# Two small float32 matmuls of an attention turned into float32r ones

## The chip, the core and the metric

One core of a Trainium2 chip runs the whole program. The metric is the device time of one execution in microseconds (us). Each engine has its own list of instructions and works through it in order; semaphores make one engine wait for another. PE is TensorE (PEld its weight loads), DVE is VectorE, ACT is ScalarE, POOL is GpSimd, SP issues DMAs. PE reads SBUF and writes PSUM alone.

## The reference, cut to what matters

Two perceiver layers on x (8 batches x 64 rows x 512), with a context of 8 x 1601 x 512. The change lies in the first attention of the first layer (32 heads of 128, 8 KV heads):

```python
q = (query @ Wq + bq).reshape(B, L, NKV, G, HDIM)
k_, v_ = jnp.split(kv @ Wkv + bkv, 2, axis=-1)
...
scores = jnp.einsum('blkgd,bmkd->bkglm', q, k) * scale
attn = jax.nn.softmax(scores, axis=-1)
o = jnp.einsum('bkglm,bmkd->blkgd', attn, v).reshape(B, L, NHEAD * HDIM)
return o @ Wo + bo
```

After it come a state-space block (mamba), a ternary linear layer, a second attention to the context, a causal self-attention and a gated feed-forward layer, each added to x.

## The kernel before, in words

**Units.** The first attention runs over 64 units, a unit being a pair (batch b, KV head i). A unit has 4 heads x 64 rows = 256 query columns and 1601 keys in 13 blocks of 128 (the last of 65). `x_all` (L517) writes out their order by hand, in six steps s = 0..5 per unit: in step s the current unit gets key projections (`x_k`, L354), value projections (`x_v`, L319) and scores (`x_s`, L369), while the unit before it gets its maximum (s = 0), exponentials (`x_exp`), values (`x_av`, L454) and at s = 5 its output (`x_o`). Two units are thus under way at any time. A scheduler then orders each engine's list from this text by its own model of the time; each list is fixed before the program runs.

**Precision.** Most matrices are held as a pair hi, lo of float32r tiles. `split` (L100) makes them: ACT copies the source to hi (L105, or L108 with a bias), another engine subtracts hi from the source for lo (L106, L109). A product is then three float32r matmuls (hi hi, hi lo, lo hi). Some small matmuls are float32 instead; among them are the two in question, the products of the exponentials with the values (L464) and parts of the mamba.

**The maximum.** Scores stand with keys on partitions and queries along the columns. `x_s` copies them from PSUM to an S tile (ACT, L388) and keeps an elementwise maximum `mx` over the key blocks (DVE, L392, L395). `x_max` (L397) transposes `mx` on PE (L403) into PSUM tile `m_ps`, and DVE reduces it to the column `mc` of negated maxima, one for each query (L405). `x_spread` (L408) brings it back along the columns on all partitions: for each of the two halves of 128 queries, a matmul with the column, broadcast, as the stationary operand and the identity as the moving one (L412), 128 columns wide, in float32. `x_exp` adds the spread maximum to S (DVE, L426) and takes the exponential (ACT, L427).

**The sum.** POOL adds up the exponentials into `ss` (L429, L452, L446) and its two halves into `sl` (L448), which holds a partial sum for each partition. In the very last unit (`flush`) DVE does part of it (L434 to L442). `x_o` (L466) adds over the partitions and spreads the result with one float32 matmul with a matrix of ones, 256 columns wide, into the second half of PSUM tile `o_ps` (L472). The reciprocal follows (L474 to L477), then the product with the values (L479), bias and split (L485).

**Buffers that matter.** PSUM: `kv` has four buffers for k_ps, v_ps, s_ps and w_ps, `o_ps` one, `m_ps` one. SBUF: `ss`, `sl`, `mx` and `rw` one each, `S` eleven, `mc` two. Pool `xw` holds the two `x1` tiles in which a pair of batches' result is gathered (`x_wo`, L492).

**Beside it.** Side work is fed into the units at given rates: splitting weights (`halves`), preparing the later layers (`prep`), and the later layers themselves for four groups of two batches (`chain`). Its DVE, ACT and POOL instructions are pinned in program order, which is why many have the line L65. The last group's chain, with what is left of the third group's, runs alone at the end. `consts` (L147) makes the identity (POOL) and the ones at the start.

Of the kernel before, what the change touches and what calls it, by code (L numbers as in the profile page):

```python
# [8 lines left out]
FP = mybir.dt.float32  # L9
FR = mybir.dt.float32r  # L10
AF = mybir.ActivationFunctionType
ALU = mybir.AluOpType
# [4 lines left out]
P = 128  # L17
D = 512
# [60 lines left out]
class Kernel:  # L79
# [67 lines left out]
    def consts(self):  # L147
        nc, i = self.nc, self.i
        c = self.ctx.enter_context(self.tc.tile_pool(name="const", bufs=1))
        self.c = c  # L150
        self.ident = c.tile([P, P], FP, name="ident")
        make_identity(nc, self.ident)
        self.eps5 = c.tile([P, 1], FP, name="eps5")
        nc.gpsimd.memset(self.eps5, 1e-5)
        self.ones = c.tile([P, P], FP, name="ones")
        nc.gpsimd.memset(self.ones, 1.0)
        self.eps6 = c.tile([P, 1], FP, name="eps6")
        nc.gpsimd.memset(self.eps6, 1e-6)

        def ld(name, shape):  # L160
            t = c.tile(shape, FP, name="c_" + name)
            nc.sync.dma_start(out=t, in_=i[name])
            return t

        self.bq = ld("bq", [P, 32])
        self.bk = ld("bk", [P, NKV])
        self.bv = ld("bv", [P, NKV])
# [229 lines left out]
    def x_max(self, b, i):  # L397

        nc = self.nc
        m = self.mf.pop((b, i))  # L400
        ps = self.px.tile([P, 2, 256], FP, name=self.nm("m_ps"), tag="m", bufs=MB)
        for h in range(2):
            nc.tensor.transpose(ps[:, 0, h * P : (h + 1) * P], m[:, 0, h * P : (h + 1) * P], self.ident)  # L403
        col = self.sb("mc", [P, 2], pool=self.xp, bufs=2)
        nc.vector.tensor_reduce(col, ps[:, 0].rearrange("p (h k) -> p h k", k=P), AX.X, ALU.max, negate=True)  # L405
        self.mm[(b, i)] = (ps, col)

    def x_spread(self, b, i):  # L408

        ps, col = self.mm[(b, i)]  # L410
        for h in range(2):
            self.nc.tensor.matmul(  # L412
                ps[:, 1, h * P : (h + 1) * P], lhsT=col[:, h : h + 1].to_broadcast([P, P]), rhs=self.ident, start=True, stop=True
            )

    def x_exp(self, b, i, n):

        nc = self.nc
        ps = self.mm[(b, i)][0]
        S = self.S[(b, i)]  # L420
        if n == 0:
            self.ss[(b, i)] = self.sb("ss", [P, 2, 256], pool=self.xp, bufs=1)
        ss = self.ss[(b, i)]
        r, w = (P, 2) if n < 6 else (TAIL, 1)
        sv = S[n][:r, :w]
        nc.vector.tensor_tensor(sv, sv, ps[:r, 1:2].to_broadcast([r, w, 256]), ALU.add)  # L426
        nc.scalar.activation(sv, sv, AF.Exp, scale=ISC)  # L427
        if n == 1:
            nc.gpsimd.tensor_tensor(ss, S[0], S[1], ALU.add)  # L429
        elif n > 3 and self.flush:  # L430

            if n == 5:
                t = self.fs = self.sb("rw", [P, 256], pool=self.xp, bufs=1)
                nc.vector.tensor_tensor(t, S[4][:, 0], S[4][:, 1], ALU.add)  # L434
                for k in range(2):
                    nc.vector.tensor_tensor(t, t, S[5][:, k], ALU.add)
            elif n == 6:
                t = self.fs
                nc.vector.tensor_tensor(t[:r], t[:r], sv[:, 0], ALU.add)
                l = self.sb("sl", [P, 256], pool=self.xp, bufs=1)  # L440
                nc.vector.tensor_tensor(l, ss[:, 0], ss[:, 1], ALU.add)
                nc.vector.tensor_tensor(l, l, t, ALU.add)  # L442
                self.l[(b, i)] = l
                self.mm.pop((b, i))
        elif n == 6:
            nc.gpsimd.tensor_tensor(ss[:r, 0], ss[:r, 0], sv[:, 0], ALU.add)  # L446
            l = self.sb("sl", [P, 256], pool=self.xp, bufs=1)
            nc.gpsimd.tensor_tensor(l, ss[:, 0], ss[:, 1], ALU.add)  # L448
            self.l[(b, i)] = l
            self.mm.pop((b, i))  # L450
        elif n > 1:
            nc.gpsimd.tensor_tensor(ss, ss, S[n], ALU.add)  # L452
# [13 lines left out]
    def x_o(self, b, i):  # L466

        nc = self.nc
        ps = self.o.pop((b, i))
        self.S.pop((b, i))  # L470
        r = self.l.pop((b, i))
        nc.tensor.matmul(ps[:, 1], lhsT=self.ones, rhs=r, start=True, stop=True)  # L472
        w = self.sb("rw", [P, 256], pool=self.xp, bufs=1)
        nc.scalar.activation(r, ps[:, 1], AF.Ln)  # L474
        nc.scalar.activation(r, r, AF.Exp, scale=-1.0)
        nc.vector.tensor_tensor(w, ps[:, 1], r, ALU.mult)
        nc.vector.scalar_tensor_tensor(r, w, 2.0, r, ALU.subtract, ALU.mult, reverse0=True)  # L477
        oa = w
        nc.vector.tensor_tensor(oa, ps[:, 0], r, ALU.mult)  # L479

        odd = b % 2
        oav = oa.rearrange("p (g t) -> p g t", t=T)
        scr = self.ot_s[b // 2][i]
        ot = self.sb("ot", [P, 2, G, 2, T], FR, pool=self.xp, bufs=OTB)
        self.split(ot[:, 0, :, odd], ot[:, 1, :, odd], oav, bias=self.bv[:, i : i + 1])  # L485
        if odd:
            nc.sync.dma_start(out=ot[:, :, :, 0].bitcast(FP), in_=scr)
            self.ot[(b, i)] = ot
        else:
            nc.sync.dma_start(out=scr, in_=ot[:, :, :, 0].bitcast(FP))  # L490
# [794 lines left out]
    def run(self):  # L1285
        nc, tc, ctx = self.nc, self.tc, self.ctx
# [2 lines left out]
        self.pc = ctx.enter_context(tc.tile_pool(name="pc", bufs=2, space=PSUM))  # L1289
        xctx = ctx.enter_context(ExitStack())  # L1290
        self.px = xctx.enter_context(tc.tile_pool(name="px", bufs=2, space=PSUM))
        self.consts()
        self.scratch()
        self.xw = ctx.enter_context(tc.tile_pool(name="xw", bufs=2))
        self.xp = xctx.enter_context(tc.tile_pool(name="xp", bufs=2))
        qctx = ctx.enter_context(ExitStack())
        self.q_ln(qctx.enter_context(tc.tile_pool(name="qp", bufs=2, side="right")))
# [192 lines left out]
```

## Time and profile before

| | |
|---|---|
| three timed runs, median (lowest to highest) | 2689.3 us (2683.2 to 2691.5) |
| the profiled execution | 2687.2 us, its span 2685.1 us |
| mean granted PE clock in it | 0.983 |
| first L472, last L472 | 108.4 us, 2375 us |
| L403, transposes of mx (PE) | 128 records, 25.3 us, 274 ns each |
| L405, reduction to mc (DVE) | x64, median 418 ns |
| L448, sum l (POOL) | x63, median 738 ns |
| L452, additions of exponentials (POOL) | x254, 349.3 us, median 1290 ns |
| L474, logarithm of the sum (ACT) | x64, median 386 ns |
| PE's idle time before L472 | 0.0 us |
| PE's idle time before L412 | 3.0 us, until DVE's mc |
| DVE's idle time before L426 | 20.5 us, of which 20.2 until PE's L412 |

How to read it. A row of a group gives the count, the busy time as the union of its instructions, the mean of one in ns, and the idle time of the engine just before them with what ended it. Matmuls overlap on PE: the mean of one record includes its drain, the busy time of a group does not count the overlap twice. A row of the chain gives the start in us, the length in us, and the engine, tile and line; "x12" counts records. A stage's row gives busy us and the count of each engine, then the granted clock of PE, the share of the DMA engines and their GB/s.

### The profile page before, as it was taken

To read this page: it belongs to the slowest core of one execution; us is meant where nothing else is said; L and a number is where in the kernel's file an instruction comes from. 1 tells how busy PE (TensorE), PEld (TensorE's weight loads), DVE (VectorE), ACT (ScalarE), POOL (GpSimd) and SP (SyncE) were. 2 spreads that over 40 slices of the span, in tenths; PEclk is the share of its full clock that TensorE was granted. 3 is DMA by queue.
4 is the path that set the end of the run, shared out by engine and by line. 5 is a ranking of instruction groups with operands and counts; after the bars stand their busy time and mean duration, and the time that the engine had idled before them with its cause. 6 is when DMAs were issued, how large, how long until landed. Compare 5 with 4: busy or idle time off the path is not lost.

```text
span 2685.1 us, 43976 instructions
## 1 busy us (share of the span) xinstructions
PE 2549.7 (95%) x16320; PEld 2269.3 (85%) x16320; DVE 1667.6 (62%) x2739; ACT 1350.2 (50%) x3128; POOL 1247.6 (46%) x1243
## 2 busy tenths in 40 slices
PE   7999999999999999999999999999999999977797
PEld 6988999999999899978989988988898898964544
DVE  4534357665687775545567676554657777668754
ACT  4545454344556554544555554544546545436433
POOL 2434463463368663521367457521239556405420
PEclk9999999999999999999999999999999999987899
DMA  9788876675213244764324452665343455466674
GB/s 308 225 295 276 281 239 190 203 240 180 67 66 105 68 133 150 232 190 145 97 98 148 149 161 89 216 201 164 102 135 92 137 159 155 143 226 216 234 261 166
DMA packets 311126, 466.08 MB, mean 174 GB/s; under 512 B 88440, under 2 KB 187768, under 8 KB 306432
## 3 DMA queue, kind: packets, MB, share of 16 engines
q1 hardware_dynamic: 310912, 463.28, 53.4%
q8 instruction: 128, 2.10, 0.3%
q14 instruction: 86, 0.70, 0.1%
HBM read 389.66 MB, written 73.53 MB: 173 GB/s over the span
## 4 chain that ended last, share of the span: by engine, by line
PE 68%; DMA 9%; DVE 9%; POOL 7%; issue 4%; ACT 3%; SPq 0%; POOLq 0%; DVEq 0%; ACTq 0%
PE v_ps L334 16%; PE k_ps L363 16%; PE o_ps L464 10%; PE s_ps L385 8%; POOL a L65 3%; PE w_ps L511 2%; PE acc L274 2%; DVE a L65 2%; PE acc L1077 2%; PE acc L801 2%; PE acc L1021 1%; PE acc L759 1%; PE acc L756 1%; POOL ss L452 1%; DMA b<-in_ctxT_dram 1%
## 5 line engine op out<-in xcount | busy, mean ns | idle before, releaser
L363 PE MATMUL k_ps<-cxb,wk 128*128 128x384 f32 x2304 | 470.3, 347 | 35.3 <-DVE mx L392 13.2
L334 PE MATMUL v_ps<-wv,cxb 128*128 128x256 f32 x3456 | 467.9, 281 | 1.0 <-DVE kt L109 0.6
L334 PEld LDWEIGHTS v_ps<-wv,cxb 128*128 128x128 f32 x3456 | 438.0, 188 | 19.3 <-issue 11.7
L363 PEld LDWEIGHTS k_ps<-cxb,wk 128*128 128x128 f32 x2304 | 405.3, 191 | 53.2 <-DVE mx L392 15.6
L464 PE MATMUL o_ps<-S,v 128*128 128x256 f32 (+1 forms) x1664 | 413.6, 381 | 7.4 <-DVE rw L479 4.0
L385 PE MATMUL s_ps<-q,kt 128*128 128x256 f32 (+1 forms) x2496 | 413.7, 299 | 5.2 <-DVE mx L392 2.4
L385 PEld LDWEIGHTS s_ps<-q,kt 128*128 128x128 f32 (+1 forms) x2496 | 342.8, 185 | 28.5 <-issue 6.9
L388 ACT COPY S<-s_ps 128x512 f32<-128x512 f32 (+1 forms) x448 | 241.9, 553 | 241.0 <-PE s_ps L385 236.6
L452 POOL TENSOR_TENSOR ss<-ss,S 128x512 f32<-128x512 f32 x254 | 349.3, 1375 | 14.7 <-ACT S L427 1.3
L392 DVE TENSOR_TENSOR mx<-s_ps,mx 128x512 f32<-128x512 f32 x256 | 175.1, 684 | 264.0 <-ACT S L388 262.7
L464 PEld LDWEIGHTS o_ps<-S,v 128*128 128x128 f32 (+1 forms) x1664 | 298.6, 190 | 46.7 <-issue 5.2
L429 POOL TENSOR_TENSOR ss<-S,S 128x512 f32<-128x512 f32 x64 | 84.5, 1320 | 469.4 <-ACT S L427 469.1
L108 ACT ACTIVATE kt<-k_ps,c_bk 128x384 fp32r<-128x384 f32 (+1 forms) x256 | 152.0, 594 | 246.9 <-PE k_ps L363 245.9
L426 DVE TENSOR_TENSOR S<-S,m_ps 128x512 f32<-128x512 f32 (+1 forms) x448 | 257.3, 640 | 20.5 <-PE m_ps L412 20.2
L427 ACT ACTIVATE S<-S 128x512 f32<-128x512 f32 (+1 forms) x448 | 246.7, 599 | 43.4 <-DVE S L426 42.7
L109 DVE SCALAR_TENSOR_TENSOR kt<-k_ps,c_bk,kt 128x384 fp32r<-128x384 f32 (+1 forms) x256 | 160.9, 629 | 158.0 <-ACT kt L108 156.5
L337 ACT COPY v<-v_ps 128x256 f32<-128x256 f32 (+1 forms) x416 | 152.5, 368 | 198.4 <-PE v_ps L334 196.0
L334 PE MATMUL v_ps<-wv,cxt 128*128 128x256 f32 (+1 forms) x1536 | 206.5, 282 | 1.5 <-DVE mx L392 1.0
L334 PEld LDWEIGHTS v_ps<-wv,cxt 128*128 128x128 f32 (+1 forms) x1536 | 192.7, 175 | 10.5 <-issue 3.4
L65 DVE TENSOR_TENSOR_SCAN a<-a,a 128x512 f32<-128x512 f32 x96 | 154.7, 1613 | 62.9 <-POOL a L65 62.8
L363 PE MATMUL k_ps<-cxt,wk 128*128 128x450 f32 x768 | 178.6, 375 | 1.4 <-DVE mx L392 1.3
L65 POOL TENSOR_TENSOR a<-a,bc 128x512 f32<-128x512 f32 x96 | 128.1, 1335 | 90.7 <-DVE a L65 90.7
(357 smaller groups left out, 3947.8 us busy)
## 6 DMA issues: line engine op xcount, KB each, us to landing
wo<-d_wo SPq DMA_DIRECT2D x128, 512.0 KB, 5.3
wk<-d_wk SPq DMA_DIRECT2D x63, 512.0 KB, 3.5
wv<-d_wv SPq DMA_DIRECT2D x31, 1024.0 KB, 5.7
cst<-in_ctxT_dram SPq DMA_DIRECT2D x96, 192.0 KB, 3.0
b<-in_ctxN_dram SPq DMA_DIRECT2D x36, 512.0 KB, 3.7
d_q<-q_t SPq DMA_DIRECT2D x32, 512.0 KB, 5.9
q<-d_q SPq DMA_DIRECT2D x64, 256.0 KB, 3.1
d_wo<-wo SPq DMA_DIRECT2D x32, 512.0 KB, 5.7
```

What stands on the lines that cost most here:

```text
L65: return lambda *a, **k: self.tc.keep_in_program_order(f(*a, **k))
L109: eng.scalar_tensor_tensor(lo, src, bias, hi.bitcast(FP), ALU.add, ALU.subtract)
L334: nc.tensor.matmul(ps[:r], lhsT=cx[:, a, c, o : o + r], rhs=w[:, m, c, :], start=k == 0, stop=k == 11)
L337: nc.scalar.copy(vt[:r], ps[:r])
L363: nc.tensor.matmul(ps[:, :wd], lhsT=w[:, a, c, :], rhs=cx[:, m, c, :], start=k == 0, stop=k == 11)
L385: nc.tensor.matmul(sp[:r, gi, :], lhsT=kt[:, a, o : o + r], rhs=q[:, m, :], start=k == 0, stop=k == 2)
L388: nc.scalar.copy(s[:r, :n], sp[:r, :n])
L392: nc.vector.tensor_tensor(mx, sp, S[0] if len(S) == 1 else mx, ALU.max)
L426: nc.vector.tensor_tensor(sv, sv, ps[:r, 1:2].to_broadcast([r, w, 256]), ALU.add)
L427: nc.scalar.activation(sv, sv, AF.Exp, scale=ISC)
L452: nc.gpsimd.tensor_tensor(ss, ss, S[n], ALU.add)
L464: nc.tensor.matmul(ps[:, 0], lhsT=self.v[(b, j, t)][:r, hc : hc + P], rhs=S[t // 2][:r, t % 2], start=t == 0, stop=t == NT - 1)
```

## The change

Three parts. The column `mc` becomes a float32r tile, and L412 multiplies it by a float32r view of the identity. The sum l is split into float32r halves hi and lo (ACT's copy, then POOL's subtraction; DVE's in the last unit), and `x_o` adds them up by two float32r matmuls with ones that accumulate in the same PSUM tile. hi and lo take a new tile with the tag `ss`, of which there is one buffer. So that identity and ones exist in float32r, the identity is made in a tile of pool `xw` and copied by ACT; the ones are made from it by DVE. Float32 users see both through a bitcast. Pool `xw` is opened earlier for that.

```diff
+        one = self.xw.tile([P, D], FP, name="one", tag="x1")[:, :P]
+        make_identity(nc, one)
+        self.ident_r = c.tile([P, P], FR, name="ident")
+        self.ident = self.ident_r.bitcast(FP)
+        nc.scalar.copy(self.ident_r, one)
...
+        self.ones_r = c.tile([P, P], FR, name="ones")
+        self.ones = self.ones_r.bitcast(FP)
+        nc.vector.tensor_scalar(self.ones_r, self.ident, 0.0, 1.0, ALU.mult, ALU.add)
...
-        col = self.sb("mc", [P, 2], pool=self.xp, bufs=2)
+        col = self.sb("mc", [P, 2], FR, pool=self.xp, bufs=2)
...
-                ps[:, 1, h * P : (h + 1) * P], lhsT=col[:, h : h + 1].to_broadcast([P, P]), rhs=self.ident, start=True, stop=True
+                ps[:, 1, h * P : (h + 1) * P], lhsT=col[:, h : h + 1].to_broadcast([P, P]), rhs=self.ident_r, start=True, stop=True
...
+                sr = self.ss[(b, i)] = self.sb("ss", [P, 2, 256], FR, pool=self.xp, bufs=1)
+                self.split(sr[:, 0], sr[:, 1], l)
...
+            sr = self.ss[(b, i)] = self.sb("ss", [P, 2, 256], FR, pool=self.xp, bufs=1)
+            self.split(sr[:, 0], sr[:, 1], l, eng=nc.gpsimd)
...
-        nc.tensor.matmul(ps[:, 1], lhsT=self.ones, rhs=r, start=True, stop=True)
+        sr = self.ss.pop((b, i))
+        for h in range(2):
+            nc.tensor.matmul(ps[:, 1], lhsT=self.ones_r, rhs=sr[:, h], start=h == 0, stop=h == 1)
```

## What was predicted

> **What bounds the kernel now.** I read the page's busy times first, then the busy time by stage, the chain of work that ended last in order of time, and the groups by line and shape for the two kinds of matmul that the change touches.
>
> ```profile
> span 2685.1 us, 43976 instructions
> PE 2549.7 (95%) x16320; PEld 2269.3 (85%) x16320; DVE 1667.6 (62%) x2739; ACT 1350.2 (50%) x3128; POOL 1247.6 (46%) x1243
> ```
>
> TensorE (PE) is busy for 95% of the span and the next engine, VectorE, for 62%. That is a mean over stages, so here are stages, as "busy (instructions)" of PE, weight loads, DVE, ACT and POOL:
>
> ```profile
> 400.00:800.00 400.00, 396.81 (x2658) 377.81 (x2657) 270.44 (x484) 190.79 (x420) 184.20 (x187) 1.00 0.50 158
> 1600.00:2000.00 400.00, 390.30 (x2547) 347.59 (x2547) 236.82 (x402) 195.22 (x458) 161.34 (x162) 1.00 0.47 153
> 2376.00:2686.00 310.00, 244.66 (x1344) 155.66 (x1344) 200.14 (x378) 141.81 (x377) 89.91 (x97) 0.88 0.67 226
> ```
>
> From 400 to 2000 us PE idles about 2% and ACT and POOL have half their time left. Matmul time saved in the first attention should therefore be time saved, as long as nothing new makes PE wait. The last 310 us have no first attention in them, and PE idles there for a fifth.
>
> ```profile
> L412 PE MATMUL m_ps<-ident,mc 128*128 128x128 f32 x256 | 40.0, 277 | 3.0 <-DVE mc L405 3.0
> L472 PE MATMUL o_ps<-sl,ones 128*128 128x256 f32 x128 | 38.2, 380 | 0.0
> ```
>
> Each of the 64 units (batch, KV head) issues two float32 matmuls on L412 and one on L472. That is 128 and 64, and the rows count 256 and 128: a float32 matmul leaves two records. The last number but one is the length of one record with its drain, which overlaps the next, so it is no price. A price is the spacing in a dense run; the chain in order of time gives it as start, us, what, records:
>
> ```profile
> 1484.19 2.11 PE k_ps L363 x12
> ...
> 1936.42 2.73 PE v_ps L334 x24
> ...
> 2223.84 2.16 PE o_ps L464 x10
> ...
> 2525.34 2.68 PE acc L941 x24
> ```
>
> float32r with 256 columns (L334): 2.73/24 = 114 ns each; with 384 (L363): 2.11/12 = 176. float32 with 256 columns (L464): 2.16/10 = 216 a record, 432 a matmul. float32 with 128 columns (L941): 2.68/24 = 112 a record, 224 a matmul.
>
> **The change part by part.**
>
> *The sum (L472).* Per unit one float32 matmul of 256 columns (432 ns) becomes two float32r ones of 256 (2 x 114 = 228). 204 ns x 64 = **13.1 us** less PE time.
>
> *The spread (L412).* Per unit two float32 matmuls of 128 columns (2 x 224) become two float32r ones of 128. No float32r matmul narrower than 256 columns is in the trace. From above its price is 224, if it gains nothing. From below it is half of L334's 114, 57: from 256 to 384 columns the price grows in proportion. Between them stands the weight load, which does not shrink with the columns streamed: a load record takes 188 ns for 128 columns (L472) and 134 for 65 (the last s_ps of a unit), so 63 columns cost 54 ns and 128 cost some 110. No two 128x128 matmuls or transposes in a run lie closer than 108 ns (L403, L412). I take 110, the row nearest in shape. Saving: 114 ns x 128 = **14.6 us**, ends 0 and 21.4.
>
> A rule that would price this otherwise is in the Trainium skill, "TensorE: Matmul & The Clock Gate", section "Back-to-back issue gap": a sustained stream of weight loads and matmuls is put there at about 81 ns per matmul for 128 columns and 131 for 512. By 81 this part would save 18.3 us (an estimate from that page) instead of 14.6. The same rule's 131 ns for 512 columns does not agree with this trace, where dense L274 matmuls of 512 columns start 228 ns apart, so I keep the row.
>
> *The split, and PE's wait for it.* After L448 (the sum l, on POOL), ACT copies l to hi (L474, same shape, 386 ns) and POOL subtracts (like L448, 738), some 1.3 us with hand-offs, then both matmuls. Paired in time, l ended before L472 began by 0.4 to 23 us, median near 10; four units have under 1.3 us (0.40, 0.77, 1.21, 1.23), nine under 2.5. The order of the built programs puts the pair of matmuls where L472 stood among first-attention matmuls for 57 of 64 units. With 1.3 us the shortfall is some 1.6 us in all, with 2.5 (a queue in front of each step) some 9. I take **3 us lost**. POOL's 63 x 738 = 47 us and ACT's 64 x 386 = 25 us of new work fit into their idle half.
>
> *ACT held up.* The copy waits for POOL, and ACT takes its list in order: behind it stand S<-s_ps, v<-v_ps and kt<-k_ps (L388, L337, L108), for which PE's ring of four "kv" buffers waits. I laid the new ACT order over the old times. In the first 32 units ACT reaches the copy before l is there 22 times, mostly by 0.1 to 3.7 us, once by 9; the next ACT instruction would start late by 22 us in all, 8 of it in unit 22. Doubled for 64 units: 44 us at worst. The ring holds three more groups of 0.7 to 2.1 us of matmuls, which covers delays up to about 3 us, so all but the longest are hidden. I take **5 us lost**, ends 0 and 44.
>
> *The ring of one for ss.* hi and lo take the ss buffer, so the next unit's first addition (L429) waits for both matmuls. In the trace L429 starts 7 us or more after the previous L472 in 61 of 63 pairs; twice it is 1 to 3 us ahead of it. POOL is not the bound: nothing.
>
> *The start.* The identity now passes through ACT. POOL has it at 1.5 us, ACT's table load ends at 2.0, the copy can end before 2.5; x arrives at 4.9 us and the first transpose is at 13.7. Nothing. Moving pool xw earlier shifts addresses alone. One "x1" buffer is used once before its first real use, long released.
>
> *The last unit.* Its sum is on DVE; L472 waits 1.6 us behind an L758 that waits for a DMA, which covers copy and subtraction (0.4 + 0.4). Nothing.
>
> *What moves.* 36 matmuls of the third group's chain, ahead of the last unit's L472 before, now stand behind it: 20 float32r ones of 512 columns (228 ns) and 16 float32 of 128 (224), 8.2 us. They leave the full stage for one in which PE has a fifth free, so the effect lies between -8.2 and, if they delay that chain instead, about +8. I take 0.
>
> **Sum:** -13.1 - 14.6 + 3 + 5 = -19.7 us. The profiled execution took 2687.2 us (span 2685.1), 2 us below the median of the three timed runs, 2689.3. 2687.2 - 19.7 = 2667.5; I predict **2667 us**. About 0.3% (8 us) is what a measurement of this kernel can tell from no change.
>
> **Rivals.**
>
> 1. *The narrow float32r matmul gains nothing* (224 ns at 128 columns). For it: no row shows a narrow one. Against: the prices of 256, 384 and 512 columns are in proportion. It gives 2687.2 - 13.1 + 8 = 2682, within 0.3%.
> 2. *ACT's line becomes the bound: slower.* Its place is the copy of l to hi; every instruction behind it on ACT waits for POOL's slow additions (1.29 us each), and PE runs out of its four buffers. It decides once PE loses more than 27.7 us by it. At the worst end, 44 us, with the 3 of the late matmuls, it gives 2687.2 - 27.7 + 47 = 2706. For it: ACT would wait in two of three units. Against: most of these waits are shorter than what the ring covers, and the order was not the same in the later units.
> 3. *Everything hides:* 57 ns, no stalls, and the moved matmuls fall into idle time: 2687.2 - 13.1 - 21.4 - 8.2 = 2644.
>
> **Chances.** The forecast (2655 to 2679) 0.58; rival 1 0.19; rival 2 0.16; rival 3 0.07. Faster by over 0.3% is forecast and rival 3, 0.65; within 0.3% rival 1, 0.19; slower by over 0.3% rival 2, 0.16. The range, 2650 to 2690, takes in the forecast and rival 1 and leaves out most of rivals 2 and 3.
>
> **What would show it.** L472's line should have 128 records 114 ns apart, and L412's 128 instead of 256. If L412's pairs lie about 110 apart the spread is right; at 224, rival 1. Idle time of PE before L472 "until POOL" is the late split. Idle time of ACT that ends with POOL's sl, together with PE waits on "ACT S" or "ACT kt", is rival 2. The stages from 400 to 2000 us should stay 97% full on PE with fewer us in each. The prediction is wrong if PE's idle time before 2376 us grows by more than 8 us, or if the last stage becomes longer than 310 us.

## The result and the profile after

The changed kernel takes **2694.5 us** (median of 13 runs, 2689.5 to 2700.4); the kernel before, on the same chip, 2688.3 us (13 runs). The ratio is 1.0024, 95% interval 1.0015 to 1.0034: no gain, and if anything a small loss, where 2667 us was predicted. The profiled execution took 2697.6 us.

Line numbers have moved by four to ten: L412 is now L416, L448 is L454, L464 (values) L472, L472 (the sum) L482, L511 L521, L759 L769, L801 L811, L812 L822. The page's total, then its stages:

```profile
span 2695.6 us, 43902 instructions
PE 2543.5 (94%) x16192; PEld 2256.3 (84%) x16192; DVE 1681.6 (62%) x2741; ACT 1371.3 (51%) x3193; POOL 1290.5 (48%) x1305
```

The 128 records fewer are the spread's: the change is in. But PE's busy time fell by only 6 us. The stages, columns as before (busy us and count of PE, PEld, DVE, ACT, POOL, granted clock, DMA share, GB/s):

```profile
400.00:800.00 400.00, 394.84 (x2645) 376.33 (x2644) 276.70 (x488) 196.74 (x440) 192.97 (x200) 1.00 0.49 157
1600.00:2000.00 400.00, 392.52 (x2580) 350.73 (x2579) 234.21 (x396) 200.43 (x474) 171.37 (x177) 1.00 0.47 148
2000.00:2376.00 376.00, 344.47 (x2145) 307.94 (x2144) 257.39 (x379) 189.66 (x466) 218.58 (x228) 0.96 0.43 136
2376.00:2696.00 320.00, 249.67 (x1337) 156.74 (x1336) 200.73 (x374) 141.28 (x374) 89.40 (x97) 0.85 0.66 219
```

And the third of these stages in the kernel before:

```profile
2000.00:2376.00 376.00, 357.05 (x2287) 324.73 (x2285) 261.35 (x381) 193.38 (x470) 221.29 (x227) 0.99 0.44 137
```

Up to 2000 us all is as predicted: PE as full as before, and further along. In the third stage PE has 142 matmuls fewer to do and is busy for 12.6 us less; that time is now idle, and nothing has moved into it. The two lines of the change, and the copy to hi, in groups by line and shape:

```profile
L482 PE MATMUL o_ps<-ss,ones 128*128 128x256 f32 x128 | 28.2, 290 | 2.1 <-ACT ss L105 1.3 <-POOL ss L106 0.6
L105 ACT CAST ss<-sl 128x256 fp32r<-128x256 f32 x64 | 25.9, 405 | 82.0 <-POOL sl L454 81.9
L416 PE MATMUL m_ps<-ident,mc 128*128 128x128 f32 x128 | 22.4, 255 | 1.1 <-DVE mc L409 0.9
```

The two matmuls of L482 wait 2.1 us in all for the split, and ACT waits 82 us in front of its copy. The price of a pair is read from the starts of matmuls: from the first record of the pair to the start of the sixth matmul behind it, less the usual spacing of the five between, median over the units with no gap. That takes in what the follower pays.

| per unit | before | after | difference x 64 |
|---|---|---|---|
| sum (L472, then L482) | 426 ns | 241 ns | -11.8 us |
| spread (L412, then L416) | 454 ns | 226 ns | -14.6 us |

Together -26.4 us, where -27.7 was predicted. Other choices of the usual spacing change each price by some 10 ns. Within a pair the starts are not where the prediction looked for them: the two L482, where they are neighbours, start 121 ns apart (median), the two L416 only 60 ns. The matmul after the second L416 then starts 112 ns behind it, and the one after that comes some 55 ns later than usual, so 226 ns is the price of the pair and not a spacing.

Gaps of over 0.3 us between matmul starts, beyond the usual spacing, from 80 us to the last sum, add up to 55.8 us before and 60.7 after: 5 us lost, where 8 was predicted. The sums depend on what is taken as usual (other choices give 63 to 88 us), and the loss lies between 0 and 7 us. By these numbers the first attention should end some 20 to 26 us earlier; its last sum starts at 2346.1 us instead of 2375.3, 29 us earlier (52 records of side work, of 1468, went behind it). **The whole gain is there at 2346 us.** From the last sum to the end, the kernel before needs 310 us and the changed one 349.5.

What happens there, in order of time (start us, us, engine, line, idle time of the engine before it and its releaser), in the changed kernel; these are chosen rows, with others between them:

```profile
2360.47 0.69 DVE L524 TENSOR_TENSOR x<-w_ps,x 128x512 f32<-128x512 f32 x1 [10.70 <-PE w_ps L521]
...
2368.49 0.63 PE L768 MATMUL acc<-w,a 128*128 128x512 f32 x1
2371.81 0.80 PE L768 MATMUL acc<-w,a 128*128 128x512 f32 x1 [1.84 <-DMA w<-d_wout]
2375.61 0.79 PE L768 MATMUL acc<-w,a 128*128 128x512 f32 x1 [2.15 <-DMA w<-d_wout]
2379.12 0.79 PE L768 MATMUL acc<-w,a 128*128 128x512 f32 x1 [1.86 <-DMA w<-d_wout]
2379.71 0.63 PE L769 MATMUL acc<-w,a 128*128 128x512 f32 x1
2380.45 0.21 POOL L822 MEMSET xpad<- 128x6 f32 x4 [40.06 <-PE acc L769]
2380.99 0.68 DVE L141 BATCH_NORM_STATS2 ln_st<-x 128x6 f32<-128x512 f32 x1
2386.23 3.65 PE L811 MATMUL acc<-a,w 128*128 128x128 f32 x22
```

L524 gives the last group's x, the end of the first attention: ready at 2361.2. Its next reader, the layer norm (L141), starts at 2381.0, and the last group's chain multiplies from 2386.2. What it waits for shows on POOL: a memset (L822), which reads nothing, waits 40 us for PE's L769. That is the third group's mamba, the last matmul of its out-projection (L766 to L769), which ends at 2380.3. A memset can only wait for the memory it writes. Once the first attention is over, a new pool `tp` opens for the last stage in the place of pool `ca`, which held the mamba's tiles: `actx.close()`, then `tile_pool(name="tp")` in `run`. So the last group's chain waits for the third group's mamba. (On DVE, L141 also stands in the list behind an addition of the third group that waits for the same L769; the experiments on memory below tell the two apart.) In the kernel before, the same two instructions:

```profile
2384.91 0.21 POOL L812 MEMSET xpad<- 128x6 f32 x4 [7.62 <-DMA b<-in_ctxT_dram]
2385.56 0.69 DVE L141 BATCH_NORM_STATS2 ln_st<-x 128x6 f32<-128x512 f32 x1
```

There the mamba ended at 2375.2 and x was ready at 2385.5: x was later, by 10 us. The DMA that this row names as the releaser landed just before the memset, but it need not be the one waited for: the last matmul of the first attention (L511) had ended too, and DVE's addition to x, which waits for that one, starts at 2384.83, 0.08 us before the memset. After the change, where both wait for L769, the memset starts as closely behind DVE's instruction (0.07 us, 2380.45 against 2380.38). So L511 fits as well; in the built programs the matmul that the memset waits for is this L511 before, and the mamba's last L769 after.

After the change x is 24 us earlier, and the mamba 5 us later. It does not follow the units: the last 16 of the mamba's 32 scans on DVE start 8 to 14 us later than before, while the units beside them run 26 to 34 us earlier. And its end is not PE's work. In the chain of work that ended last (start us, us, what), of the stretch from 2340 to 2392 us:

```profile
2345.24 2.63 DMA w<-d_wout
...
2369.15 2.62 DMA w<-d_wout
2371.77 0.04 issue
2371.81 0.81 PE acc L768
2372.62 0.02 issue
2372.64 2.93 DMA w<-d_wout
2375.57 0.04 issue
2375.61 0.81 PE acc L768
2376.42 0.02 issue
2376.44 2.64 DMA w<-d_wout
```

Load a slice of the weight, multiply for 0.8 us, free the buffer, load the next. The same view gives DMA w<-d_wout 20.8% of this stretch. Meanwhile PE is busy for half of the time and DVE for a quarter; the stretch from 2346 to 2386 us:

```profile
2346.00:2386.00 40.00, 20.87 (x73) 14.20 (x73) 10.33 (x28) 6.28 (x19) 1.47 (x5) 0.64 0.53 170
```

### The profile page after: what moved, and what is told of

Read it like the earlier page. It is cut to its first block, busy times and chain, and to the rows that moved or that the text cites. A ratio compares the mean times of both kernels' runs of the same rounds, so it can differ in the third digit from the quotient of the medians.

```text
span 2695.6 us, 43902 instructions
## 1 busy us (share of the span) xinstructions
PE 2543.5 (94%) x16192; PEld 2256.3 (84%) x16192; DVE 1681.6 (62%) x2741; ACT 1371.3 (51%) x3193; POOL 1290.5 (48%) x1305
## 4 chain that ended last, share of the span: by engine, by line
PE 64%; DVE 10%; DMA 9%; POOL 9%; issue 5%; ACT 3%; SPq 1%; POOLq 0%; DVEq 0%; ACTq 0%
PE v_ps L338 15%; PE k_ps L367 15%; PE o_ps L472 9%; PE s_ps L389 8%; POOL a L65 3%; DVE a L65 3%; PE w_ps L521 2%; PE acc L278 2%; POOL ss L460 2%; PE acc L1087 2%; PE acc L811 2%; PE acc L1031 2%; PE acc L766 2%; PE acc L769 1%; DMA wo<-d_wo 1%
## 5 line engine op out<-in xcount | busy, mean ns | idle before, releaser
L367 PE MATMUL k_ps<-cxb,wk 128*128 128x384 f32 x2304 | 463.7, 343 | 31.0 <-DVE mx L396 11.3
L338 PEld LDWEIGHTS v_ps<-wv,cxb 128*128 128x128 f32 x3456 | 440.5, 189 | 26.4 <-issue 16.3
L367 PEld LDWEIGHTS k_ps<-cxb,wk 128*128 128x128 f32 x2304 | 399.0, 190 | 48.4 <-issue 11.5
L472 PE MATMUL o_ps<-S,v 128*128 128x256 f32 (+1 forms) x1664 | 413.0, 381 | 1.6 <-DVE rw L489 1.6
L472 PEld LDWEIGHTS o_ps<-S,v 128*128 128x128 f32 (+1 forms) x1664 | 300.5, 190 | 36.6 <-DVE rw L489 2.0
```

The source lines that it names most:

```text
L338: nc.tensor.matmul(ps[:r], lhsT=cx[:, a, c, o : o + r], rhs=w[:, m, c, :], start=k == 0, stop=k == 11)
L367: nc.tensor.matmul(ps[:, :wd], lhsT=w[:, a, c, :], rhs=cx[:, m, c, :], start=k == 0, stop=k == 11)
L472: nc.tensor.matmul(ps[:, 0], lhsT=self.v[(b, j, t)][:r, hc : hc + P], rhs=S[t // 2][:r, t % 2], start=t == 0, stop=t == NT - 1)
```

## The experiments

What the expectations call theory A: the third group's chain keeps a pace of its own, and the last stage is held by its mamba, so that TensorE time freed in the first attention is not time saved. Rivals are named in each. All times are medians; a ratio is to the kernel before on the same chip and in the same call, whose medians lie between 2687.7 and 2691.0 us.

### Each part alone

Here e1_spread keeps the float32 sum, e2_sum the float32 spread, and e3_consts has only the new way to make identity and ones.

```diff
 # e1: the column and L416 as in the change, L472 and its sum as before
 # e2: the split and L482 as in the change, L412 and mc as before
 # e3: only consts() and the earlier opening of pool xw
```

> The spread by float32r alone, the sum as before. Theory A (the first attention gets shorter, but the third group's mamba, which runs beside it and is not bound by TensorE, keeps its own pace, and the end of the program hangs on it): the last sum matmul comes some 14 us earlier than in the kernel before (2361 against 2375 us), the time stays within 5 us of 2688. Theory B (the split's copy and subtraction, with ScalarE and GpSimd waiting for each other, slow that mamba; less TensorE work alone is a gain): 2672 to 2677 us. Theory C (any edit moves the scheduler's order, and the order alone moves the end by some us): no pattern with the edit.

> The split sum alone, the spread in float32 as before. Theory A: the last sum matmul 13 us earlier (2362), the time within 5 us of 2688. Theory B: slower than the kernel before, 2692 to 2702 us, since it has all of the added waits and half of the saving. Theory C: no pattern.

> Only the constants made as in the change (identity through ScalarE, pool opened earlier), the attention as before. Theories A and B: 2688, within 2 us. Theory C: it differs by more than 4 us, for it too gives the scheduler another text.

e1 takes 2705.0 us, 1.0055 (1.0040 to 1.0070); e2 2718.2, 1.0109 (1.0092 to 1.0125); e3 2689.2, 1.0002 (0.9992 to 1.0012). The constants cost nothing, as predicted. The prices hold alone: the spread 228 ns a unit in e1, the sum 241 in e2. Yet both are slower, outside the ranges of theories A and B, and e1 adds no work in the units. The third group's mamba ends at 2391.9 us in e1 and 2400.4 in e2, against 2375.2 before, and from there to the end of the span it is 311 and 322 us, against 310 before: the end follows the mamba, as theory A says, but theory A did not foresee a later mamba. Why it ends later still than in the whole change was not settled.

### ACT's wait taken away

The copy to hi moves to POOL, which has made l itself, so ACT no longer waits for it.

```diff
-            self.split(sr[:, 0], sr[:, 1], l, eng=nc.gpsimd)
+            nc.gpsimd.tensor_copy(sr[:, 0], l)
+            nc.gpsimd.tensor_tensor(sr[:, 1], l, sr[:, 0].bitcast(FP), ALU.subtract)
```

> The whole change, but GpSimd makes both halves of the sum (copy, then subtraction), so ScalarE no longer waits for GpSimd's sum nor GpSimd for ScalarE's copy. Theory B: ScalarE's 82 us of waiting for the sum go, and the time falls to 2670 to 2682 us. Theory A: 2688 to 2700 us, as the whole change. GpSimd has some 0.7 us more work for each of 63 units.

2694.3 us, 1.0012 (1.0000 to 1.0024), the time of the change itself. The ss tile's waits in the changed kernel (engine, tile, line: us, times):

```profile
  POOL sl L454: 81.9, 48
```

In e4 this line is gone (one copy is left on ACT, of the last unit), and nothing is gained at the end. That alone does not clear ACT's line (rival 2 of the prediction), for e4's first attention ends later than the change's: its last sum starts at 2365.6 us, with 44 more records of side work ahead of it, and one wait of 9.7 us on PE. What speaks against rival 2 is the changed kernel itself, whose PE loses 0 to 7 us in the units where that rival needs over 27.7. For theory A e4 is a point: the last sum moves by 19 us against the change and the end does not, while the mamba ends at 2377.3 us (2380.3 in the change) and the last chain starts 6 us behind it.

### The rate of the third group's chain

`SPAN` holds the due time of each group's chain, in batches of the first attention; the third's goes from 2.6 to 2.5 or 2.4, with and without the change; e12 takes all three down.

```diff
-SPAN = [3.1,3.1,2.6,0.2]
+SPAN = [3.1,3.1,2.5,0.2]
```

> The whole change, with the third group's chain fed in over 2.5 instead of 2.6 batches, so that its mamba stands some 20 us earlier in the lists. Theory A (the last group's chain can start only when that mamba has ended, and the end follows it by 305 to 322 us, whatever the first attention does): mamba end near 2360 instead of 2380, the time 2668 to 2682 us. Theory D (the last stage is bound by the work left to it, and what is moved ahead lengthens the units by as much): within 5 us of 2694.

> The kernel before over 2.5 batches. There the mamba's end (2375 us) and the first attention's last projection (2385 us) nearly coincide, so under theory A little is to be had: 2680 to 2692 us. Theory D: the same. If it falls to 2670, the gain of the whole change with this setting is not the change's.

> The same over 2.4 batches. Theory A: the mamba ends before the first attention does (2350 to 2360 us), the time 2655 to 2675 us. Theory D: within 8 us of 2694.

> The kernel before over 2.4 batches. Theory A: 2675 to 2692 us, above the whole change at the same setting by some 15 us or more.

> The whole change with the chains of all three groups fed in somewhat faster (3.0, 3.0 and 2.5 batches instead of 3.1, 3.1 and 2.6). Theory A: the mamba's end moves ahead to about 2350 to 2360 us and the time falls below the kernel before, 2670 to 2685 us. Theory C: any value from 2680 to 2720.

At 2.5 the changed kernel takes 2687.0 us, 0.9992 (0.9983 to 1.0000), and its control 2700.4, 1.0036 (1.0023 to 1.0048): the change is now worth 13 us. At 2.4 both are slow: 2719.1, 1.0104 (1.0088 to 1.0119), and 2728.1, 1.0139 (1.0125 to 1.0153). e12 takes 2728.3, 1.0145 (1.0117 to 1.0172). All five lie above the ranges of theory A. One reason is that a smaller `SPAN` does not mean an earlier mamba: it ends at 2360 us at 2.5, but at 2381 (e6) and 2385 at 2.4, and at 2404.6 in e12, where 2350 to 2360 was expected of e6 and e12. The other is that the expectation of a fixed 305 to 322 us from the mamba's end to the end of the span, which the kernel before, the changed one, e1, e2 and e9 kept, did not hold in e5 to e8 (327 to 341).

### Less TensorE work by another road

e9 is the kernel before with the last of the twelve matmuls of each value block left out (L333): 416 matmuls of 114 ns, some 48 us of PE. Neither the sum nor the spread is touched.

```diff
-            for a, m in ((0, 0), (0, 1), (1, 0)):
+            for a, m in ((0, 0), (0, 1), (1, 0))[: 2 if c == NC - 1 else 3]:
```

> The kernel before, with the last of the 12 matmuls of every value block left out (lo times hi of the last quarter of the contraction): 416 x 116 ns = 48 us less TensorE work in the first attention and nothing added anywhere. Theory A (the side chain keeps its own pace and sets the end): the last sum matmul some 48 us earlier (2327), the time no more than 15 us less (2673 to 2690). Rival E (the units' matmul time does bound the kernel, and the change lost its gain to what it adds): 2638 to 2652 us.

2694.3 us, 1.0007 (0.9994 to 1.0019). Its last sum starts at 2337.2 us, 38 earlier than before, and its x is ready 32 us earlier, at 2353.0; nothing of it arrives at the end. The same two readings as after the change:

```profile
2374.70 0.21 POOL L812 MEMSET xpad<- 128x6 f32 x4 [42.73 <-PE acc L759]
2375.24 0.68 DVE L141 BATCH_NORM_STATS2 ln_st<-x 128x6 f32<-128x512 f32 x1
```

The mamba ends at 2374.6 us, within 1 us of the kernel before (2375.2), and the memset waits 43 us for it. The last chain starts at 2380.6 us, only 11 us before that of the kernel before, and these 11 us are lost again behind it. This is the strongest run for theory A: the change's own parts play no role in it.

### A shorter mamba

Half of the scan steps of the third group are left out, with the change (e10) and without (e11).

```diff
-                bc = bcast(sh)
+                bc = bcast(sh) if gi != 2 or sh < 2 else None
...
+                    if gi == 2 and sh >= 2:
+                        yield 4
+                        continue
```

> The whole change, with half of the 32 scan steps of the third group's mamba left out (states 8 to 15), everything else at its place in the text. Theory A: that mamba is no longer late, the last group's chain starts after the first attention's own end (2360), and the time is 2655 to 2675 us. Theory C (the scheduler's order of the last stage varies by more than this): no lower than 2685 us.

> The kernel before with the same half left out, as the control. Theory A: there the first attention ends at 2385 us and binds, so 2676 to 2690 us, 15 to 28 us above the whole change with the same left out: that difference is what the change is worth when the side chain does not hold the end. Theory C: no such difference.

e10 takes 2649.9 us, 0.9845 (0.9820 to 0.9870), e11 2676.2, 0.9935 (0.9917 to 0.9953). The mamba ends at 2335.9 and 2317.5 us, long before x is there, and the change is worth 26.3 us: with the mamba out of the way, what TensorE saves comes out at the end. (e10 is below theory A's range, e11 at its lower edge; their difference is within what was expected, 15 to 28 us.)

### The memory gate

The tail's tiles get fewer buffers, so that pool `tp` fits beside the mamba's memory. The mamba keeps its length.

```diff
 # e13, e14: s4 8, w2 6; e15 to e18:
-BUFS_TAIL = {... "s4": 11, ... "w2": 12, ...}
+BUFS_TAIL = {... "s4": 6, ... "w2": 10, ...}
 # e17, e18 also: SPAN = [3.1,3.1,2.5,0.2]
```

> The whole change, with the last stage's pool made 24 KB per partition smaller (tag s4 8 instead of 11 buffers, w2 6 instead of 12), so that it fits into the memory that the first attention leaves and no longer covers that of the third group's mamba. If the last group's chain waits for that mamba because of the memory (theory A1), its projections start some 6 us after the first attention's last one, near 2368 instead of 2386 us, and the time falls by 5 to 18 us, less what the missing weight buffers cost. If it waits because of the order of the lists or of the third group's chain sharing the engines (theory A2), the start stays near 2386 or the end does not follow.

> The kernel before with the same smaller pool, as the control: there the first attention's end (2385 us) sets the start, so theory A1 expects no gain, only the price of the fewer buffers: 2688 to 2700 us.

> The whole change with the 24 KB taken elsewhere (s4 6, w2 10). Theory A1: start near 2368 as well; the time differs from the other by the price of the buffers alone, within 10 us.

> The kernel before, with the last stage's buffers cut as in e15_after_tp2 (s4 11 to 6, w2 12 to 10), so that its pool fits beside the mamba's memory. Theory A (the last group's chain was held by the third group's mamba through memory, and in the kernel before by the first attention's end, which lies 10 us later anyway): the control starts its last chain at 2390 to 2398 us, as the kernel before (2391.8), and gains little, 2683 to 2694 us; the change is then worth 2 to 12 us under these buffers. Rival (the smaller buffers only gave the scheduler a luckier order of the last stage): the control gains as much as e15 gained on the changed kernel, about 12 us, and lands at 2674 to 2682.

> The whole change with the buffers of e15_after_tp2 and the rate of the third group's chain of e5_after_span25 (SPAN[2] 2.6 to 2.5). If the two gates are cleared independently, the mamba of the third group ends some 20 us earlier than in e15 (near 2370 instead of 2390), the last chain still starts near 2366, and the two chains share the engines for less time at the end: 2665 to 2680 us. If the order of the last stage decides, as it did at other rates, no gain over e15 (2682) or a loss, up to 2700.

> The control to e17_after_tp2_span25: the kernel before with the same two edits (s4 6, w2 10; SPAN[2] 2.5). Theory A: TensorE's list of the first attention, not the third group's mamba, sets the start of the last chain (last L472 near 2378 us, mamba end near 2362, start near 2394), so the 27 us of TensorE time are worth nearly all they are worth in e10/e11 and e15/e16: 2695 to 2710 us, 18 to 33 above e17. Rival (the pair e15/e16 was luck of the last stage's order): a difference below 10 us, 2677 to 2687.

The last group's chain in e15:

```profile
2361.96 0.69 DVE L524 TENSOR_TENSOR x<-w_ps,x 128x512 f32<-128x512 f32 x1 [11.55 <-PE w_ps L521]
2362.04 0.21 POOL L822 MEMSET xpad<- 128x6 f32 x4 [21.00 <-DMA w<-d_wout]
2362.69 0.69 DVE L141 BATCH_NORM_STATS2 ln_st<-x 128x6 f32<-128x512 f32 x1
...
2367.42 5.02 PE L811 MATMUL acc<-a,w 128*128 128x128 f32 x28 [0.68 <-ACT a L725]
```

The layer norm follows x at once, and the chain multiplies from 2367.4, though the mamba ends at 2390.4. So the wait was one for memory and not for data, and not for the order of the lists alone, since only buffers were changed. (The memset again starts 0.08 us behind DVE's addition to x, which waits for L521; the DMA named there fits no better than that matmul.) The times, with the last sum's start, the mamba's end and the last chain's start in each profiled execution:

| pair: change / control | last sum | mamba ends | last chain starts | time, us | ratio (95%) |
|---|---|---|---|---|---|
| as is: after | 2346.1 | 2380.3 | 2386.2 | 2694.5 | 1.0024 (1.0015-1.0034) |
| before | 2375.3 | 2375.2 | 2391.8 | 2688.3 | |
| SPAN 2.5: e5 | 2344.6 | 2360.2 | 2366.0 | 2687.0 | 0.9992 (0.9983-1.0000) |
| e7 | 2376.5 | 2360.1 | 2396.2 | 2700.4 | 1.0036 (1.0023-1.0048) |
| SPAN 2.4: e6 | 2340.7 | 2380.9 | 2386.8 | 2719.1 | 1.0104 (1.0088-1.0119) |
| e8 | 2369.9 | 2384.7 | 2390.7 | 2728.1 | 1.0139 (1.0125-1.0153) |
| half mamba: e10 | 2352.4 | 2335.9 | 2374.7 | 2649.9 | 0.9845 (0.9820-0.9870) |
| e11 | 2373.6 | 2317.5 | 2395.7 | 2676.2 | 0.9935 (0.9917-0.9953) |
| w2 6: e13 | 2343.9 | 2385.9 | 2364.4 | 2705.5 | 1.0056 (1.0038-1.0073) |
| e14 | 2379.7 | 2379.7 | 2396.2 | 2696.9 | 1.0023 (1.0010-1.0035) |
| w2 10: e15 | 2346.7 | 2390.4 | 2367.4 | 2682.1 | 0.9970 (0.9959-0.9980) |
| e16 | 2383.5 | 2383.5 | 2400.6 | 2708.7 | 1.0073 (1.0056-1.0089) |
| w2 10, SPAN 2.5: e17 | 2344.4 | 2361.1 | 2362.7 | 2676.7 | 0.9951 (0.9935-0.9966) |
| e18 | 2376.0 | 2359.1 | 2395.5 | 2708.2 | 1.0083 (1.0061-1.0104) |

The three columns of points in time are those of the profiled execution, which can lie up to 11 us from the median (e10: 2660.5 us). The pairs e15 with e16 and e17 with e18 ran on different chips; by their ratios the change is worth 28 and 35 us there.

In every pair the change ends the first attention 21 to 37 us earlier. Where its last chain starts at most 6 us before its control's (as is, SPAN 2.4), it is worth between +6 and -9 us. Where it starts 21 to 33 us before, it is worth -13, -26, +9, -27 and -32 us: four of five have a gain, and e13, with half the w2 buffers, has not. In e13 the chain starts 22 us earlier than in the changed kernel, as theory A said, but then needs 335 us instead of 309, and the fall of 5 to 18 us that was expected did not come. e18 was at the upper edge of theory A's range, and e16 outside every range: the control itself lost 20 us to the smaller tail (e16 was expected at 2683 to 2694), 9 of them before its last chain starts and the rest after; why was not settled. The pair shows what the change is worth under these buffers, not what the smaller tail is worth. e17 beats both kernels, by 12 us the one before and by 18 the changed one, and e15 by 8 and 12, on their medians; without the change the same edits cost 20 us.

## Why the prediction was wrong

**The step that failed** is the one from busy to bound: "Matmul time saved in the first attention should therefore be time saved, as long as nothing new makes PE wait." PE was 97% busy and nothing new of weight made it wait, and the time was still not saved: e9 takes 48 us of matmuls away and changes nothing (1.0007, 0.9994 to 1.0019). A second path of almost the same length ran beside it, the third group's chain, whose end the units' matmul time does not set (2374.6 us in e9, 2375.2 before). Before, the two met at the last stage 10 us apart (mamba 2375.2, x 2385.5). So at most about 10 us of an earlier x could show, however much was saved: e9 makes x 32 us earlier and the last chain's start 11. That was to be read before. In the kernel before, the chain of work that ended last, of the stretch from 2350 to 2393 us:

```profile
2359.57 0.23 PE acc L758
2359.80 0.03 PE acc L759
2359.83 2.56 DMA w<-d_wout
...
2366.90 7.53 DMA w<-d_wout
2374.43 0.04 issue
2374.48 0.50 PE acc L758
2374.97 0.24 PE acc L759
```

At 2367 the chain leaves the first attention and goes through 7.5 us of a transfer for the third group's mamba. Even the last sum, at 2375.3, stood behind that L758 in PE's list. The prediction mentions this very L758, as cover for the split in the last unit, and did not ask why PE, the engine it called the bound, was waiting there.

**What moves: "I take 0", bounds -8.2 to +8** had the right place and the wrong frame. I asked what 36 moved matmuls weigh in the last stage. The question was when that stage may start, and how far the third group's work is ahead of it. From the last chain's start to the end, the changed kernel takes 309 us and the one before 293: the third group's output leaves at 2689.7 instead of 2668.8, so the two groups share the engines to the end. That the earlier start of 5.6 us and these 16 us make up the +10 us of the two profiled executions (2697.6 and 2687.2) is arithmetic; why the order costs 16 us is not shown. The granted clock was lower, 0.86 from 2386 us on against 0.89 from 2392 before; how much of the 16 us that is stays open.

**The prices held.** The sum: 13.1 predicted, 11.8 measured. The spread: 14.6 predicted, 14.6 measured; 226 ns a unit is 113 a matmul, next to the 110 that the weight-load row gave. So rival 1 (224) is false for this width, and so is the end of 57 ns as a price. The sign that was named for it misled: the two L416 start 60 ns apart, near that end, and the rest of the price falls on the matmuls behind them. The 81 ns that the Trainium skill, "TensorE: Matmul & The Clock Gate", section "Back-to-back issue gap", gives per matmul for a sustained stream at 128 columns is not what these pairs cost (113); no run here has a longer stream of float32r matmuls this narrow.

**The waits held.** PE's lost time grew by 5 us (0 to 7, by what is taken as usual), where 3 + 5 were taken. ACT's waits were there, 81.9 us of idle time in front of the copy in 48 of 64 units, and were hidden but for part of these few us at most. The ring of one for ss, the start and the last unit cost nothing that shows (e3: 1.0002).

**The rivals.** Rival 2 had the sign and not the cause: its price was a loss on PE in the units, and there was none of that size. No rival had the real one, a second path that takes over at the end. The text did name its sign: "if the last stage becomes longer than 310 us".

**What stays open.** Why e1 and e2 end the third group's mamba 12 to 20 us later than the whole change does, and what makes the last chain 279 to 335 us long from one order of the same work to the next. Each list is written anew for every kernel, so single pairs carry some 10 to 20 us of this (an estimate, from the spread of the pairs). Over the five pairs whose last chain the change lets start early, the mean gain is 18 us, with one loss of 9 among them: that the saving can reach the end is shown, its size is not.

## What to carry to other kernels

A busy share near 100% says that an engine has no room, not that its time is the kernel's: before pricing a saving, find the first instruction of the stage behind it and list everything that it needs, memory too, with the time at which each was there. The second latest of these caps the gain, as the mamba did here. A cheap probe is to leave some work out of the busy engine: if the time does not move, another path has the end. And when an instruction that reads nothing waits, look for whose memory it was given.

## What the runs showed of the hardware

In the pairs of L416 a float32r matmul of 128 columns cost 113 ns, as against 114 for one of 256 columns in the dense value projections. By these two rows half the columns saved nothing, and the gain of the narrow one over float32 (two records of 112 ns) comes from one record instead of two. That the weight load sets this floor fits the load records, which are as long for 128 columns streamed as for 256 (188 and 189 ns), but no run varies the load alone.

The granted clock fell where PE was left waiting: 0.64 from 2346 to 2386 us in the changed kernel. The 512-column matmul L768 has records of 0.63 to 0.80 us there. e15, whose last chain fills that stretch, has:

```profile
2346.00:2386.00 40.00, 28.43 (x148) 23.02 (x148) 21.84 (x64) 16.04 (x47) 0.65 (x8) 0.83 0.84 292
```

That is 148 matmuls instead of 73, at 0.83; its L768 at 2372.5 takes 0.39 us. So here the emptier TensorE was also the slower one, and its busy time in the last stage rose with fewer matmuls (249.7 us for 1337 after, 244.7 for 1344 before, over the same 320 us). Whether the waiting lowers the clock, or something else in that stretch does, no run separates.
